# A linear-attention and sparse-FFN kernel: the attention's instruction order planned for all five engines, its q and k/v products interwoven, its division moved to ScalarE

## The chip, the cores and the metric

The kernel runs on one core of a Trainium2 chip. A core has a matrix engine (TensorE, PE in the profile), VectorE (DVE), ScalarE (ACT), GpSimd (POOL) and SyncE (SP), which here only issues DMAs. Each engine takes its instructions in the order in which the program was built, and waits where an operand isn't there yet; whatever stands behind the waiting instruction waits too. Matrix products are written to PSUM, eight banks of 128 x 512 float32 words; everything else lies in SBUF or in DRAM. The metric is the device time of one execution, in microseconds.

## What is computed

All values are float32. The input x has 2 batches of 1,024 positions with 512 features. The first layer is causal linear attention, the second an FFN whose hidden values are thinned 2 of 4; each is put between two layer norms and added to its input.

```python
q, k, v = xn @ Wq.T, xn @ Wk.T, xn @ Wv.T        # 16 query heads, 4 k/v heads, 128 wide
q, k = rope(q), rope(k)
qf, kf = elu(q) + 1, elu(k) + 1
state += kf outer v;  z += kf                     # running over the positions
out = (qf @ state) / (qf . z + 1e-6)
x = x + layernorm(out @ Wo.T)
h = silu(xn2 @ w_gate) * (xn2 @ w_up)             # 2,048 wide
h = h with the two largest of every four kept
x = x + layernorm(h @ w_down)
```

## The kernel before

**Tiling.** The attention runs in 16 steps, numbered `n`. A step takes 128 positions of both batches (`c = n % 8`) and one half of the heads (`n // 8`, two passes). Inside a step there are four groups `i`, each one batch with one k/v head and its four query heads. The FFN follows in four blocks of 512 positions.

**Products.** Each 2 x 2 block product (q, k/v, o, gate, up, down) is made with seven multiplications instead of eight, in the helper `strassen` (L121). It uses three PSUM banks: `cb` gathers products 1, 6, 7, 4; `ca` holds product 2; `ce` gathers 5 and 3. Between two products into `cb`, ScalarE copies the bank out (`keep`, L133), and VectorE later adds the copies to the other banks (L142, L155, L162). The next product into the same bank must wait for the copy. In the attention the banks come from one pool of four (`ps_mm`); transposes have a bank of their own (`ps_tr`), scores one (`ps_sc`), and the attention's numerators and denominators two (`ps_nm`).

**A step.** `kv_products(n)` and `q_products(n)` make k, v and q (L635), and `features` applies rope on VectorE (L656, L662), adds on GpSimd (L668), and makes elu + 1 with a relu and an exponential on ScalarE (L670, L671) and one VectorE operation (L672). A q block is then turned into the layout of its heads: `turned` transposes 32 x 32 blocks on VectorE (L581), `store_blocks` writes 256 KB to DRAM (L588), `load_blocks` reads them back in four DMAs (L593). `scores(n, i)` multiplies k and q (L740) and masks on VectorE (L749). `attend(n, i)` multiplies with the state and with v (L765, L766), makes the addition to the state (L769), and divides on VectorE (L771 to L774). Its result goes the same way through DRAM (`ob`), and `o_sums` and `o_products(n - 1)` make the output projection (L838) a step later. In the second pass both passes' outputs are added, normed and written to DRAM as `x2`.

**Preparation.** The seven-product scheme needs sums of weight blocks. Those of the second pass and of the FFN are made during the attention by `prepare` in small parts, one part per call of `first(i)`: it loads a unit of 1 MB on SyncE, makes four additions on GpSimd (L497 to L501), and stores seven pieces.

**What sets the order.** The attention runs inside `manual_schedule` for PE, Pool and SP: for these three engines the order is that of the program text, which is written out by hand with generators (`run(qpr, 2)` advances the q chain by two products). VectorE and ScalarE are left to the framework's scheduler, as are all engines in the FFN. In a step the order of the products is q1 q2 q6 q5 q7, attend, score, q4 k1 q3 k2 k6 k5 k7, attend, score, k4 k3, o1 o2 o6, attend, score, o5, the k transpose, o7, attend, score, o4 o3. The last FFN-like work inside the attention are two `gate` chains (`early`), which fill the last step.

Of the kernel before, what the change touches and what calls it, by code (L numbers as in the profile page):

```python
# [31 lines left out]
FACTORS = {1: (0, 0), 2: (1, 1), 3: (4, 2), 4: (2, 6), 5: (6, 3), 6: (3, 4), 7: (5, 5)}  # L32


@with_exitstack
def kernel(
# [369 lines left out]
    ps_mm = left("ps_mm", 4, space=PSUM)  # L406
    ps_tr = left("ps_tr", 1, space=PSUM)
# [74 lines left out]
    def prepare(units):  # L482


        loaded = prepare_load(*units[0])
        written = None
        yield
        for n in range(len(units)):
            (a11, a12, a21, a22), dst = loaded
            if written:  # L490
                written()
            for k, a in enumerate((a11, a12, a22)):
                nc.sync.dma_start(out=dst(k), in_=a)
            yield
            if n + 1 < len(units):
                loaded = prepare_load(*units[n + 1])
            nc.gpsimd.tensor_tensor(a22, a21, a22, ALU.add)  # L497
            nc.gpsimd.tensor_tensor(a21, a11, a21, ALU.subtract)
            yield
            nc.gpsimd.tensor_tensor(a11, a22, a11, ALU.subtract)  # L500
            nc.gpsimd.tensor_tensor(a12, a12, a11, ALU.subtract)  # L501

            def written(dst=dst, sums=(a11, a12, a21, a22)):
                for k, a in enumerate(sums):
                    nc.sync.dma_start(out=dst(3 + k), in_=a)

            yield
        written()

# [34 lines left out]
    def prepare_all():  # L544
        yield from sums(wo_sb, nc.gpsimd)
        units = []
        for quarter, t, parts in (
            (kv_quarter, wkv_dram, (slice(0, 2),)),
            (q_quarter, wq_dram, (slice(0, 1), slice(1, 2))),
            (o_quarter, wo_dram, (slice(0, 2), slice(2, 4))),  # L550
        ):
            for part in parts:
                units.append((quarters(quarter, part), view_quarters, part_of(t, part)))
        for jb in range(NJB):
            for i, w in enumerate((w_gate, w_up)):
                units.append((whole(columns(w, jb)), view_gu, into_gu(gu_dram[jb][i])))
        for jb in range(NJB):
            of = w_down[jb * 512 : (jb + 1) * 512, :].rearrange("(p r) o -> p r o", r=4)
            units.append((whole(of), view_d, into_d(jb)))
        yield from prepare(units)  # L560

    preparing = prepare_all()

    def transposed(src):

        t = ps_tr.tile([P, 4, P], F32, tag="tr", name="pst")
        for j in range(4):
            nc.tensor.transpose(t[:, j, :], src[:, j, :], ident)
        return t
# [7 lines left out]
    def turned(src):  # L577


        t = qp.tile([P, 4, 4, 32], F32, tag="blocks", name="blocks", bufs=4)  # L580
        nc.vector.transpose(  # L581
            out=t.rearrange("p b i r -> p i b r"),
            in_=src.rearrange("p i (b d) -> p i b d", d=32),
        )
        return t

    def store_blocks(t, to):
        nc.sync.dma_start(out=to, in_=t.rearrange("p b i r -> p (b i r)"))  # L588

    def load_blocks(t, of_):  # L590

        for b in range(4):
            nc.sync.dma_start(  # L593
                out=t[b * 32 : (b + 1) * 32],
                in_=of_.rearrange("(u d) (b e) -> b d u e", u=4, b=4)[b],
            )

    xf = {}

    def step_normalize(n):  # L600
        xns = []
        for b in range(B):
            mean, rs = layernorm_scale(xt[n][:, b, :], "a")
            normalize(xt[n][:, b, :], xt[n][:, b, :], mean, rs)
            xns.append(xt[n][:, b, :].rearrange("p (c d) -> p c d", c=NIC))
        return xns

    def step_input(n, xns, batches=range(B)):

        if 0 in batches:  # L610
            xf[n] = ln.tile([P, 7, 2, P], F32, tag="xf", name="xf")
        t = xf[n]
        for b in batches:
            pt = transposed(xns[b])
            if b == 0:
                nc.scalar.copy(t[:, 0:2].rearrange("p q k d -> p (q k) d"), pt)
            else:
                nc.vector.tensor_tensor(t[:, 3], pt[:, 0:2, :], t[:, 0], ALU.subtract)
                nc.scalar.copy(t[:, 2], pt[:, 2:4, :])
        if 1 in batches:  # L620
            nc.vector.tensor_tensor(t[:, 4], t[:, 2], t[:, 3], ALU.subtract)
            nc.vector.tensor_tensor(t[:, 5], t[:, 4], t[:, 0], ALU.subtract)
            nc.vector.tensor_tensor(t[:, 6], t[:, 1], t[:, 4], ALU.subtract)
            nc.sync.dma_start(out=xf_dram[n], in_=t)

    def step_input_again(n):
        t = ln.tile([P, 7, 2, P], F32, tag="xf", name="xf")
        nc.sync.dma_start(out=t, in_=xf_dram[n - NC])
        xf[n] = t

    def project(w, x_):
        def product(bank, i, start):
            wi, xi = FACTORS[i]
            for k in range(2):
                nc.tensor.matmul(  # L635
                    bank.rearrange("p h d -> p (h d)"),
                    x_[:, xi, k, :],
# [8 lines left out]
    def strassen_a(width, product, c11, c12, c22, done):  # L646
        return strassen((ps_mm, qp), [P, width // HD, HD], product, c11, c12, c22, done)

    def features(src, n, dst):
# [4 lines left out]
        u = rawp.tile([P, 4, HD], F32, tag="u", name="u")  # L654
        r = rawp.tile([P, 4, HD], F32, tag="r", name="r")
# [6 lines left out]
        nc.vector.tensor_tensor(  # L662
            r.rearrange("p h (t d) -> p h t d", t=2),
            src.rearrange("p h (t d) -> p h t d", t=2)[:, :, ::-1, :],
            sin,
            ALU.mult,
        )
        nc.gpsimd.tensor_tensor(u, u, r, ALU.add)  # L668

        nc.scalar.activation(r, u, AF.Relu, scale=-1.0)  # L670
        nc.scalar.activation(r, r, AF.Exp, scale=-1.0)  # L671
        nc.vector.scalar_tensor_tensor(dst, u, 0.0, r, ALU.max, ALU.add)  # L672
# [3 lines left out]
    kf, kT, v1, q_blocks = {}, {}, {}, {}  # L676
    GROUPS = ((0, 0), (1, 1), (0, 1), (1, 0))

    def kv_products(n):
        raw = rawp.tile([P, 4, HD], F32, tag="raw", name="kraw", bufs=4)  # L680
# [3 lines left out]
        yield from strassen_a(  # L684
            256,
            project(weights[n // NC][0], xf[n]),
            raw[:, 0:2, :],
            raw[:, 2:4, :],
            v[:, 2:4, 0:HD],
            lambda t: nc.scalar.copy(v[:, 0:2, 0:HD], t),  # L690
        )
        f = kv.tile([P, 4, HD], F32, tag="kf", name="kf")
        features(raw, n, f)
        kf[n] = f

    def k_transposed(n):
        t = kv.tile([P, 4, P], F32, tag="kT", name="kT")
        nc.scalar.copy(t, transposed(kf[n]))
        kT[n] = t

    def q_products(n):
        raw = [rawp.tile([P, REP, HD], F32, tag="raw", name="qraw", bufs=4) for _ in range(3)]

        def feature(i, src):
            f = qp.tile([P, REP, HD], F32, tag="qf", name="qf", bufs=1)
            features(src, n, f)
            q_blocks[n, i] = turned(f)

        run = strassen_a(
            512,  # L710
            project(weights[n // NC][1], xf[n]),
            raw[0],
            raw[2],
            raw[1],
            lambda t: feature(2, t),
        )
        for i, _ in enumerate(run):
            if i == 1:
                feature(0, raw[0])
            elif i == 4:  # L720
                feature(1, raw[1])
            elif i == 6:
                feature(3, raw[2])
            yield

    state = {}
    qT, am, o, blocks = {}, {}, {}, {}

    def q_store(n, i):
        store_blocks(q_blocks.pop((n, i)), qb_dram[n % 2][i])  # L730

    def q_load(n, i):
        t = qp.tile([P, 4, P], F32, tag="qT", name="qT", bufs=4)
        load_blocks(t, qb_dram[n % 2][i])
        qT[n, i] = t

    def scores(n, i):
        b, j = GROUPS[i]
        sc = ps_sc.tile([P, 4, REP, 32], F32, tag="sc", name="sc")
        nc.tensor.matmul(  # L740
            sc.rearrange("p u h t -> p (u h t)"),
            kT[n][:, 2 * b + j, :],
            qT[n, i].rearrange("p u e -> p (u e)"),
            start=True,
            stop=True,
        )
        t = qp.tile([P, 4, REP, 32], F32, tag="am", name="am")
        mask = causal.rearrange("p (u t) -> p u t", t=32).unsqueeze(2)
        nc.vector.tensor_tensor(t, sc, mask.broadcast_to([P, 4, REP, 32]), ALU.mult)  # L749
        am[n, i] = t  # L750

    def attend(n, i):

        b, j = GROUPS[i]
        c = n % NC
        v = v1[n][:, 2 * b + j, :]
# [5 lines left out]
        for u in range(4):  # L762
            dst = nmv[:, u // 2, u % 2, :]
            if c > 0:
                nc.tensor.matmul(dst, q[:, u, :], state[b, j], start=True, stop=False)  # L765
            nc.tensor.matmul(dst, a[:, u, :], v, start=(c == 0), stop=True)  # L766
        if c < NC - 1:
# [377 lines left out]
```

## Time and profile before

| | |
|---|---|
| median of three runs | 1433.1 us (1426.0 to 1436.2) |
| profiled execution | 1429.7 us, of which the span is 1428.0 us |
| mean granted TensorE clock | 0.971 |
| TensorE busy | 1313.1 us, 92% of the span |
| VectorE, ScalarE, GpSimd busy | 892.0, 402.1, 336.0 us |
| moved by DMA | 263 MB, 184 GB/s |
| the costliest wait of TensorE | `PE cb L635 <- ACT u L133`: 27.2 us in 23 waits |

A busy matrix engine isn't an engine at its pace: matmuls are pipelined, and the time shown for one is longer than the distance to the next. The distance between two starts is what counts. The clock is given as a share of full speed; a stage at 0.5 runs its products at half speed.

### The profile page before, as it was taken

To read this page: it belongs to the slowest core of one execution; us is meant where nothing else is said; L and a number is where in the kernel's file an instruction comes from. 1 tells how busy PE (TensorE), PEld (TensorE's weight loads), DVE (VectorE), ACT (ScalarE), POOL (GpSimd) and SP (SyncE) were. 2 spreads that over 40 slices of the span, in tenths; PEclk is the share of its full clock that TensorE was granted. 3 is DMA by queue.
4 is the path that set the end of the run, shared out by engine and by line. 5 is a ranking of instruction groups with operands and counts; after the bars stand their busy time and mean duration, and the time that the engine had idled before them with its cause. 6 is when DMAs were issued, how large, how long until landed. Compare 5 with 4: busy or idle time off the path is not lost.

```text
span 1428.0 us, 17352 instructions
## 1 busy us (share of the span) xinstructions
PE 1313.1 (92%) x5888; PEld 1033.9 (72%) x5888; DVE 892.0 (62%) x1612; ACT 402.1 (28%) x698; POOL 336.0 (24%) x265
## 2 busy tenths in 40 slices
PE   5889989899789878898898999999999999999997
PEld 3456757666566566576566888888888888888886
DVE  5767875676466557667767548734774278525762
ACT  3523332232122212222232332403331242213311
POOL 5333332332233323435341220101001100110000
PEclk9889999999989999999999999999999999999999
DMA  6256666666776886676557437445553655356412
GB/s 222 93 172 202 213 207 220 197 199 205 250 259 217 248 262 190 210 243 212 182 197 257 164 126 244 140 142 207 155 154 118 229 156 153 123 173 176 113 60 89
DMA packets 200295, 263.32 MB, mean 184 GB/s; under 512 B 18448, under 2 KB 125968, under 8 KB 196112
## 3 DMA queue, kind: packets, MB, share of 16 engines
q1 hardware_dynamic: 198976, 260.38, 57.0%
q10 hardware_dynamic: 1232, 1.84, 0.4%
q8 instruction: 48, 0.79, 0.2%
q14 instruction: 39, 0.32, 0.1%
HBM read 178.52 MB, written 83.62 MB: 184 GB/s over the span
## 4 chain that ended last, share of the span: by engine, by line
PE 64%; DVE 16%; DMA 5%; ACT 5%; issue 4%; POOL 3%; SPq 3%; DVEq 0%; ACTq 0%; POOLq 0%
PE cb L237 15%; PE ce L237 8%; PE cb L346 6%; PE cb L838 6%; PE cb L635 5%; PE ca L237 4%; PE ce L346 4%; POOL u L668 3%; PE nm L766 3%; DVE blocks L581 2%; PE nm L765 2%; PE ce L838 2%; DVE r L662 2%; PE sc L740 2%; PE ce L635 2%
## 5 line engine op out<-in xcount | busy, mean ns | idle before, releaser
L133 ACT COPY u<-cb 128x512 f32<-128x512 f32 (+1 forms) x252 | 126.0, 500 | 553.4 <-PE cb L237 189.5
L668 POOL TENSOR_TENSOR u<-u,r 128x512 f32<-128x512 f32 x80 | 106.0, 1326 | 308.8 <-DVE r L662 240.4
L635 PE MATMUL cb<-wq,xf 128*128 128x512 f32 x256 | 128.5, 626 | 23.5 <-DMA xf<-xf 8.3
L838 PE MATMUL cb<-wo,of 128*128 128x256 f32 x512 | 124.9, 388 | 9.6 <-DVE of L825 8.3
L237 PE MATMUL cb<-fxt,wgu 128*128 128x256 f32 x512 | 117.8, 381 | 1.9 <-ACT u L133 1.9
L838 PEld LDWEIGHTS cb<-wo,of 128*128 128x128 f32 x512 | 97.1, 194 | 30.9 <-issue 12.3
L237 PE MATMUL cb<-fxnT,wgu 128*128 128x256 f32 x512 | 116.9, 379 | 0.0
L635 PEld LDWEIGHTS cb<-wq,xf 128*128 128x128 f32 x256 | 49.6, 199 | 83.8 <-issue 65.9
L237 PEld LDWEIGHTS cb<-fxt,wgu 128*128 128x128 f32 x512 | 96.5, 190 | 17.7 <-ACT u L133 4.4
L237 PEld LDWEIGHTS cb<-fxnT,wgu 128*128 128x128 f32 x512 | 97.2, 190 | 13.6 <-issue 0.5
L766 PE MATMUL nm<-v,am 128*128 128x129 f32 x512 | 101.0, 289 | 2.1 <-ACT state L787 2.1
L185 POOL TENSOR_TENSOR h<-h 128x512 f32<-128x512 f32 x16 | 23.3, 1459 | 332.1 <-DVE ht L182 297.4
L765 PE MATMUL nm<-state,qT 128*128 128x129 f32 x448 | 92.1, 289 | 0.0
L670 ACT ACTIVATE r<-u 128x512 f32<-128x512 f32 x80 | 50.2, 630 | 148.8 <-POOL u L668 106.3
L635 PE MATMUL cb<-wkv,xf 128*128 128x256 f32 x256 | 73.4, 413 | 19.9 <-ACT u L133 19.9
L155 DVE TENSOR_TENSOR y<-u,ce 128x256 f32<-128x256 f32 (+1 forms) x21 | 9.5, 459 | 128.3 <-ACT u L133 128.3
L672 DVE SCALAR_TENSOR_TENSOR qf<-u,r 128x512 f32<-128x512 f32 x64 | 58.2, 910 | 48.4 <-ACT r L671 43.4
L766 PEld LDWEIGHTS nm<-v,am 128*128 128x128 f32 x512 | 82.4, 206 | 3.8 <-ACT state L787 2.5
L635 PEld LDWEIGHTS cb<-wkv,xf 128*128 128x128 f32 x256 | 50.4, 203 | 47.1 <-ACT u L133 28.0
L765 PEld LDWEIGHTS nm<-state,qT 128*128 128x128 f32 x448 | 77.5, 206 | 9.2 <-issue 6.8
L740 PE MATMUL sc<-qT,kT 128*128 128x512 f32 x128 | 67.2, 607 | 1.3 <-DMA qT<-qb 1.3
L346 PE MATMUL cb<-wd,h 128*128 128x256 f32 x256 | 58.3, 381 | 4.4 <-DVE h L325 4.3
(150 smaller groups left out, 2487.1 us busy)
## 6 DMA issues: line engine op xcount, KB each, us to landing
wgu<-gs SPq DMA_DIRECT2D x112, 256.0 KB, 2.7
wgu<-us SPq DMA_DIRECT2D x112, 256.0 KB, 2.7
wd<-d_dram SPq DMA_DIRECT2D x28, 1024.0 KB, 4.9
qb<-blocks SPq DMA_DIRECT2D x64, 256.0 KB, 2.8
qT<-qb SPq DMA_DIRECT2D x256, 64.0 KB, 2.3
ob<-blocks SPq DMA_DIRECT2D x60, 256.0 KB, 3.0
of<-ob SPq DMA_DIRECT2D x240, 64.0 KB, 2.0
xf<-xf SPq DMA_DIRECT2D x16, 896.0 KB, 5.3
```

The source lines that it names most:

```text
L133: nc.scalar.copy(t, b)
L237: nc.tensor.matmul(bank[:, j, :], w[:, k, j, :], xf[xi][:, k, :], start=(start and j == 0 and k == 0), stop=(j == 1 and k == 1), skip_grou ...
L346: nc.tensor.matmul(bank[j] if split else bank[:, j, :], hf[jb][hi][:, k, j * P : (j + 1) * P], w[:, jb, k, :], start=(start and jb == 0 an ...
L581: nc.vector.transpose(out=t.rearrange("p b i r -> p i b r"), in_=src.rearrange("p i (b d) -> p i b d", d=32),)
L635: nc.tensor.matmul(bank.rearrange("p h d -> p (h d)"), x_[:, xi, k, :], w[:, wi, k, :], start=(start and k == 0), stop=(k == 1), skip_grou ...
L668: nc.gpsimd.tensor_tensor(u, u, r, ALU.add)
L670: nc.scalar.activation(r, u, AF.Relu, scale=-1.0)
L672: nc.vector.scalar_tensor_tensor(dst, u, 0.0, r, ALU.max, ALU.add)
L740: nc.tensor.matmul(sc.rearrange("p u h t -> p (u h t)"), kT[n][:, 2 * b + j, :], qT[n, i].rearrange("p u e -> p (u e)"), start=True, stop= ...
L765: nc.tensor.matmul(dst, q[:, u, :], state[b, j], start=True, stop=False)
L766: nc.tensor.matmul(dst, a[:, u, :], v, start=(c == 0), stop=True)
L838: nc.tensor.matmul(bank.rearrange("p h d -> p (h d)"), of[n, xi][:, k, :], w[:, wi, k, :], start=(start and k == 0), stop=(k == 3), skip_g ...
```

## The change

**A plan.** A class `Plan` walks through the attention when the kernel is built. It keeps a clock and, for each engine, the time from which it is free. Small generators describe what must happen after a product (`yield "dve", 0.75` means that VectorE is taken for 0.75 us; `yield "of", n, i` waits for a named event; a third element is a rank among requests of the same time). The instruction is issued to the program when its turn comes in this plan, and that fixes the order on VectorE, ScalarE, GpSimd and SyncE. TensorE's order is still written out, and `plan.pe` only moves the clock. The whole attention is now under `manual_schedule` for all five engines. Nothing of the plan is left when the kernel runs.

```diff
+class Plan:
+    def step(self):
+        t, rank, _, process, request = heapq.heappop(self.heap)
+        if request:
+            engine, length = request[:2]
+            if self.free.get(engine, 0.0) > t:
+                self.push(self.free[engine], rank, process, request)
+                return
+            t += length
+            self.free[engine] = t
+        self.now = t
+        self.go_on(process)
+    def pe(self, length, issue, *names):
+        self.need(*names)
+        start = max([self.pe_free] + [self.ready[name] for name in names])
+        self.until(start)
+        issue()
+        self.now = self.pe_free = start + length
...
-    with tc.manual_schedule(
-        engines={mybir.EngineType.PE, mybir.EngineType.Pool, mybir.EngineType.SP}
-    ):
+    with tc.manual_schedule(engines={E.PE, E.Pool, E.SP, E.DVE, E.Activation}):
```

**Banks by role.** The four banks and the transposes' one become one `a`, two `b` and two `e` banks. `chain` takes the place of `strassen` in the attention, with the same seven products in the same order; transposes of x, of k and of the last outputs use an `a` or an `e` bank.

```diff
-    ps_mm = left("ps_mm", 4, space=PSUM)
-    ps_tr = left("ps_tr", 1, space=PSUM)
+    ps_mm = left("ps_mm", 2, space=PSUM)
...
+    def bank(kind, shape):
+        bufs = 1 if kind == "a" else 2
+        k = uses[kind]
+        uses[kind] += 1
+        before = [("bank", kind, k - bufs)] if k >= bufs else []
+        plan.need(*before)
+        t = ps_mm.tile([P, 512], F32, tag=f"mm{kind}", name=f"c{kind}", bufs=bufs)
...
+        def snapshot(b, i):
+            yield "act", act, 0
+            kept[i] = keeps[0].tile(shape, F32, tag=keeps[1], name=f"u{i}", bufs=keeps[2])
+            nc.scalar.copy(kept[i], b)
+            plan.signal((*name, "kept", i))
```

**Blocks through DRAM.** Turning, storing and loading are one generator. The plan takes 0.1 us of SyncE for the store and 0.45 us for the four loads, and lets 2.6 us pass between them.

```diff
+    def moved(src, through, new, name, *names):
+        yield "dve", 0.75
+        t = qp.tile([P, 4, 4, 32], F32, tag="blocks", name="blocks", bufs=4)
+        nc.vector.transpose(
...
+        yield 0.1
+        yield "sp", 0.1
+        nc.sync.dma_start(out=through, in_=t.rearrange("p b i r -> p (b i r)"))
+        yield 2.6
+        for n in names:
+            yield n
+        yield "sp", 0.45
+        t = new()
         for b in range(4):
             nc.sync.dma_start(
```

**Division on ScalarE.** One VectorE multiplication over 128 x 512 becomes four ScalarE activations over 128 x 128, each with a column of reciprocals as its scale.

```diff
-        nc.vector.tensor_tensor(
-            t.rearrange("p (i j) d -> p i j d", i=2),
-            nmv[:, :, :, 0:HD],
-            den.unsqueeze(3).broadcast_to([P, 2, 2, HD]),
-            ALU.mult,
-        )
+            for u in range(4):
+                yield "act", 0.37
+                nc.scalar.activation(
+                    t[:, u, :],
+                    nmv[:, u // 2, u % 2, 0:HD],
+                    AF.Copy,
+                    scale=den[:, u // 2, u % 2 : u % 2 + 1],
+                )
```

**The step's order.** The q and k/v chains of the next step are interwoven product by product (the lines for steps after the first):

```diff
+            kvp, qpr = kv_products(n + 1), q_products(n + 1)
+            run(qpr, 1)
+                run(kvp, 1)
+                run(qpr, 1)
+                run(qpr, 1)
+            run(kvp, 1)
+                outputs(0)
+            run(kvp, 1)
+            run(qpr, 1)
+            run(kvp, 1)
+            run(qpr, 1)
+            run(kvp, 1)
+                outputs(1)
+                run(qpr, 1)
+                run(kvp, 1)
+                run(qpr, 1)
+                run(kvp, 1)
+                run(opr, 2)
+                outputs(2)
+                run(opr, 2)
+                k_transposed(n + 1)
+                run(opr, 1)
+            outputs(3)
```

`outputs(i)` releases one part of the preparation, then attends to group i and makes the next group's scores. The last two products of the o chain open the next step. The first step (n = 0) and the last have orders of their own; in the last, `early_gate` makes the two gate chains, interwoven with the last two o chains.

**Smaller parts.** The norms of the two batches (of the four blocks at the FFN's beginning) share one square root on ScalarE (`layernorm_pair`). `features` works in place on the raw block, with three buffers for `r`. The reloaded x factors of the second pass are requested at the start of a step, for the step after next. The second pass's weights are requested every 3.5 us of the plan once the first pass's last q (k/v) products have been issued. The FFN after the attention's end is unchanged in the text.

## What was expected of it

> **What bounds the kernel now.** I read the stages first, then the waits of TensorE, then one step of it in order of time, then SyncE's queue and its DMAs. In the stages I cut the span at the end of the start-up (88 us, where the first product of the third step's q begins), at the same product 13 steps later (733.8) and at the end of the attention's last product (848).
>
> ```profile
> 0.00:88.03 88.03, 63.16 (x195) 37.75 (x195) 58.70 (x103) 34.77 (x60) 39.04 (x33) 0.86 0.48 156
> 88.03:733.79 645.76, 578.49 (x2549) 416.65 (x2548) 426.54 (x803) 176.41 (x337) 219.84 (x176) 0.96 0.68 219
> 733.79:848.00 114.21, 106.49 (x523) 86.63 (x522) 67.43 (x149) 38.47 (x71) 22.76 (x19) 0.99 0.52 176
> 848.00:1428.00 580.00, 564.99 (x2625) 492.86 (x2623) 339.37 (x558) 152.41 (x231) 54.40 (x39) 1.00 0.49 152
> ...
> PE cb L635 <- ACT u L133: 27.2, 23, 5.5
> PE ce L635 <- DVE r L662: 14.3, 10, 2.8
> PE pst L568 <- DVE x L119: 9.6, 3, 7.8
> ```
>
> The columns of a stage are its length, the busy time of TensorE, its weight loads, VectorE, ScalarE and GpSimd, then the granted clock, the DMA share and GB/s. The last stage, 580 us, runs at clock 1.00 and back to back; the change hardly touches it, so I leave it at 580. The attention's 848 us are where something can be won. Busy time doesn't say how much, since matmuls overlap in it; I take the pace from starts in the timeline of one step.
>
> ```profile
> 143.42 1.88 PE L635 MATMUL cb<-wq,xf 128*128 128x512 f32 x4
> 145.14 0.39 PE L765 MATMUL nm<-state,qT 128*128 128x129 f32 x2
> ...
> 147.15 1.02 PE L740 MATMUL sc<-qT,kT 128*128 128x512 f32 x2
> 148.01 1.88 PE L635 MATMUL cb<-wq,xf 128*128 128x512 f32 x4
> 149.73 1.03 PE L635 MATMUL cb<-wkv,xf 128*128 128x256 f32 x4
> 150.59 1.88 PE L635 MATMUL ce<-wq,xf 128*128 128x512 f32 x4
> ...
> 154.04 1.13 PE L635 MATMUL cb<-wkv,xf 128*128 128x256 f32 x4 [0.70 <-ACT u L133]
> ...
> 157.57 1.13 PE L635 MATMUL cb<-wkv,xf 128*128 128x256 f32 x4 [1.05 <-ACT u L133]
> ...
> 163.13 0.60 PE L568 MATMUL pst<-ident,x 128*128 128x128 f32 x4
> 163.57 1.89 PE L838 MATMUL cb<-wo,of 128*128 128x256 f32 x8
> 165.30 1.89 PE L838 MATMUL ca<-wo,of 128*128 128x256 f32 x8
> ```
>
> A q product takes 1.72 us (148.01 to 149.73), a k/v product 0.86, an o product 1.73, an attend 2.01 (145.14 to 147.15), a score 0.86, four transposes 0.44. A step holds 7 of each product, 4 attends, 4 scores and one k transpose: 12.0 + 6.0 + 12.1 + 8.0 + 3.4 + 0.4 = 42.1 us, and 0.9 more where x is transposed. With the lighter attends around the change of pass (no state to read at its first step, none to write at the last) the 13 steps sum to 547 us. They took 645.8, or 49.7 a step. Of the 99 us between, the timeline's brackets add up to 67 us of waiting, and a clock of 0.96 is 26 us. So TensorE is the bound, and a seventh of the attention is waiting and the clock dips that follow it. The start-up loses 25 us to waits (9 of them before the first product, which stay) and 12 to its clock of 0.86; the tail about 10.
>
> **The clock, row and rule.** The rows show clock losses only in stages that have waits (0.86, 0.96, 0.99 against 1.00). The Trainium skill's "TensorE: Matmul & The Clock Gate", section "Why this matters for your kernels", has the clock fall to half only after an idle gap of more than some 3 us. By that rule only the long waits (5.5, 7.9 and 7.3 us, beside a few near 3) cost clock, and some 10 of the 26 us would come back. The rows speak for more: the window from 672 to 714 us has no wait above 2.8 us and a clock of 0.92. I count the clock in proportion to the waits that go, which is some 18 us of the 64 below; by the rule it would be 10, and the forecast 8 us higher.
>
> **The change, part by part.**
>
> *TensorE's order.* No product is added. What changes is how much other TensorE work lies between a product and the bank it waits for. Before, k7 came one product (k5, 0.86 us) after k6, whose copy it waits for; the copy takes 0.37 us, on a ScalarE that often stood behind an addition of GpSimd. Hence most of the 27.2 us, and the 14.3 us come from k5's bank, released by VectorE. Afterwards the steady order is q1 k1 q2 q6 k2, attend, score, k6 q5 k5 q7 k7, attend, score, q4 k4 q3 k3 o1 o2, attend, score, o6 o5, transpose, o7, attend, score, o4 o3. Between q1 and q6 lie 2.6 us, between k6 and k7 4.3, between k7 and k4 4.6. The tightest is k2 behind q2 on the one "a" bank: 1.72 us against an addition of 0.68. Two attends, which share the one nm bank pair, lie at least 6 us apart but in the first step. So the 67 us of waits lose their cause, if VectorE and ScalarE keep the planned order.
>
> *Division on ScalarE.* It takes 64 operations of 0.685 us (the o<-nm,den row, L774) off VectorE, 2.7 us a step, and VectorE falls from 426.5/13 = 32.8 to 30.1 us a step. ScalarE gets 16 a step of 128x128. The nearest row is the state copy of 128x129 out of PSUM, 0.263 us: 4.2 us, from 13.6 to 17.8 us a step. "ScalarE: Activation LUTs", section "What ACT_TABLE_LOAD costs", prices an activation with a pointer operand at 0.28 us + 0.83 ns an element, 0.39 us here: 6.2 us a step. Neither makes ScalarE a bound; I take the row. A bank copy behind four divisions is 1.1 to 1.6 us late, which the gaps above cover. Without that cover (a copy behind a relu that waits for GpSimd) it is worth 1 to 5 us each time, as the 5.5 us wait was.
>
> *Norms in pairs, fewer table switches.* One square root for two blocks saves 0.3 us of ScalarE each. Off the path; nothing.
>
> *SyncE.* This is where I expect the gain to be limited. Every q and o block goes through DRAM: a store of 256 KB, then four loads that SyncE can't issue before the store has landed.
>
> ```profile
> L593 SPq DMA_DIRECT2D of<-ob x240: 302/430/1496, 74.7 to 792.2; - x120
> ...
> SPq L588 <- DVE blocks L581: 134.1, 43, 9.8
> SPq L593 <- DMA ob<-blocks: 59.5, 24, 6.8
> ```
>
> An issue costs 0.43 us (the median in the first row), and the changed kernel has, like this one, 57.8 DMAs a step (752 in 13 steps, counted in its SyncE order): 25 to 26 us. The plan reckons 0.1 us for one and 0.45 for four. "DMA: Bandwidth & Descriptors" has the same view: its table of the fixed cost gives dispatch some 50 ns, and "Issuing engines are not separate DMA queues" calls the time to initiate usually small. By that SyncE spends 3 us a step and can't matter; by the row it spends 26. I go by the row. Worse, before only 26 of the 124 loads of a block stood four DMAs or fewer behind their store; afterwards 83 do, 44 of them directly behind it. In the 13 steps before, 24 such loads waited 59.5 us, 2.5 each. Afterwards 71 of them, 5.5 a step: 13.7 us. SyncE then needs 26 + 13.7 = 40 us of a TensorE step of 42.1. On top come its waits for VectorE's blocks, 134.1/13 = 10.3 us a step before. Those were largely spare time, and a SyncE that runs late finds its blocks done. I keep half, 5: 44.8 us a step. The bounds are 42.5 (none stays, TensorE decides) and 50.1 (all stay).
>
> *Bank roles (1 + 2 + 2 instead of 4, transposes included).* The o chain's first bank is the q chain's of the same step, released by two rope products (1.4 us) 3.4 us earlier. Covered; without cover 0 to 1 us a step, within the bounds above.
>
> *GpSimd and the preparation.* The same additions at the same one part per attend, but attends come 11 instead of 12.4 us apart, and stores of prepared weights had kept GpSimd idle up to 16.7 us. I put nothing on it, since its queue was then mostly empty; up to 1 us a step if rope additions queue behind it.
>
> *Start.* The first score needs q's first block through DRAM: 0.68 + 1.6 rope + 1.33 GpSimd + 0.63 + 1.28 table + 0.63 + 0.90 + 0.70 transpose + 3.0 store + 1.8 issues + 2.3 landing = 15 us, against 18.6 us of products that now lie between. GpSimd still makes wq's sums then (four of 2.47 us), and three VectorE operations stand ahead, so I leave a wait of 3 us and other small ones; of the 28 us lost after the first product 16 come back. The tail gives 4 of its 10.
>
> Sum: 13 x (49.7 - 44.8) = 64, + 16 + 4 = 84 us. The profiled execution took 1429.7 us (span 1428.0): 1346. The median of the runs, 1433.1, lies 3.4 above it: 1349.
>
> **Rivals.**
>
> *All waits go* (chance 0.22): SyncE's waits for VectorE vanish and steps take 42.6. 13 x 7.1 = 92, + 20 + 6 = 118: 1315. For it: one step before took 42.7 us (its second q product at 436.93, the next step's at 479.65). Against: that was the light step, without states, of 38.5 us work.
>
> *SyncE or DMA clearly the bound* (0.20): steps of 47.5, start + 8, tail 2: 39 us, 1394. For it: the DMA share, 0.68 at 49.7 us a step, would be 0.75 at 45, and landings lengthen (of 3.0 us typical, 9.7 seen).
>
> *Slower* (0.10): the waits for landings come on top of those for VectorE, none replaced, in SyncE's queue. A step is then 26 + 10.3 + 5.5 w. It reaches 49.7 plus the 20 us of start and tail (1.5 a step) at w = 2.7 us, only 0.2 over the measured 2.5. At w = 3.2, with every load directly behind its store, 53.9: 13 x 4.2 - 20 = 35 us, 1468. Against: SyncE would have to stay just as late as its producers.
>
> *The order planned isn't the order that helps* (0.06): ScalarE stands behind GpSimd as often as before and only the interleaving counts, steps of 49 and start + 2: 11 us, 1422.
>
> **How the numbers follow.** The forecast has 0.42. The range takes in the first rival down to 1305 and the second up to 1418; outside lie the slower case, half of the last, and a little below. About 1% is what a measurement of this kernel can tell from no change: faster 0.84, same 0.05, slower 0.11.
>
> **What would show it.** Right: waits of TensorE in the 13 steps under 30 us, clock 0.98 or more; SyncE's waits for ob and qb landings well over 150 us, for blocks well under 134; VectorE near 30 us a step; divisions near 0.26 us. Wrong, if TensorE waits for qT or of (SyncE the bound), or if copies still wait behind relu.

## The result, and the profile after

The changed kernel takes 1471.5 us (median of 4 runs, 1469.7 to 1473.4) where the kernel before takes 1431.6 (4 runs). The ratio is 1.028, with a 95% interval of 1.024 to 1.032: slower, where faster was forecast. The profiled execution took 1473.4 us, with a span of 1471.7.

First the stages, cut at the same places of the program as before; the columns are those of the prediction.

```profile
0.00:76.10 76.10, 55.80 (x190) 34.15 (x191) 56.40 (x89) 30.52 (x63) 39.00 (x33) 0.93 0.51 169
76.10:775.80 699.70, 586.02 (x2555) 430.26 (x2554) 407.66 (x751) 237.93 (x542) 229.72 (x178) 0.91 0.64 205
775.80:890.00 114.20, 104.92 (x513) 85.78 (x512) 64.84 (x135) 41.07 (x92) 26.27 (x20) 0.96 0.51 168
890.00:1471.70 581.70, 567.28 (x2633) 494.23 (x2632) 337.94 (x556) 154.82 (x232) 50.64 (x36) 1.00 0.49 152
```

The start became 12 us shorter. The 13 steps in the middle became 54 us longer: 53.8 us each instead of 49.7, with VectorE less busy than before and TensorE's clock down to 0.91. Tail and FFN stand where they were. So the whole loss lies in the middle, and no engine there is busier than TensorE at 84%.

Next, what TensorE waits for in the 13 steps, the costliest first: total, times, longest.

```profile
PE ca L866 <- DVE qraw L710: 61.5, 4, 20.7
PE cb L866 <- ACT u L703: 36.6, 8, 6.7
PE sc L1018 <- DMA qT<-qb: 7.9, 1, 7.9
PE cb L1186 <- ACT v L945: 5.9, 4, 2.4
```

The many short waits of before (23 of 1.2 us on copies, 10 of 1.4 on k5's bank) are gone, as forecast. In their place stand twelve long ones at the same two kinds of release: a bank that VectorE reads (L710) or ScalarE copies out (L703). Neither engine is slow; the same stretch of the waits of all engines says what holds them.

```profile
DVE of L1160 <- DMA of<-ob: 133.0, 12, 18.0
ACT o L1080 <- DVE den L1076: 129.3, 42, 9.7
...
SPq L776 <- DMA ob<-blocks: 100.9, 37, 6.6
SPq L769 <- DVE blocks L763: 99.2, 33, 10.9
SPq L776 <- DMA qb<-blocks: 73.5, 33, 5.9
```

L1160 is the first of the three sums that `o_sums` makes for the output projection. It needs the attention output of group 3, the last group of the step, after that block's way through DRAM. It was nearly always late: 12 waits in 13 steps, 11 us each (a thirteenth, 24.9 us at the change of pass, is put down to a weight load; the sums' waits in the whole execution are 158 us). In the kernel before, the same sum (L825) never waited for over 0.05 us. The rows give the wait instructions in front of it, in ns: shortest, median, longest; first the kernel before, then the changed one (one wait of VectorE can be split over several of them).

```profile
L825 DVEq EVENT_SEMAPHORE  x16: 21/35/50, 115.7 to 801.9; - x16
L1160 DVEq EVENT_SEMAPHORE  x35: 21/50/18151, 106.2 to 836.1; - x35
```

The fence before that has two more engines. ScalarE's division (L1080) waits for the reciprocals of VectorE (L1076). SyncE (L776, the four loads of a block) waits 174 us for stores to land.

One step in order of time shows how these hang together: VectorE, then TensorE, then SyncE's queue (start, length, instruction; in brackets the idle time before it and what ended it).

```profile
331.77 0.71 DVE L763 STREAM_TRANSPOSE blocks<-o 128x512 f32<-128x512 f32 x1 [0.36 <-ACT o L1080]
333.86 0.42 DVE L710 TENSOR_TENSOR y<-u,ce 128x256 f32<-128x256 f32 x1 [1.38 <-PE ce L1186]
352.23 0.69 DVE L1160 TENSOR_TENSOR of<-of 128x512 f32<-128x512 f32 x1 [17.95 <-DMA of<-ob]
352.84 0.68 DVE L710 TENSOR_TENSOR qraw<-u,ca 128x512 f32<-128x512 f32 x1
...
337.95 1.88 PE L866 MATMUL cb<-wq,xf 128*128 128x512 f32 x4
353.58 2.07 PE L866 MATMUL ca<-wkv,xf 128*128 128x256 f32 x4 [13.74 <-DVE qraw L710]
355.44 0.64 PE L1062 MATMUL nm<-state,qT 128*128 128x129 f32 x2
...
334.67 0.42 SPq L769 DMA_DIRECT2D ob<-blocks  x1
...
338.72 1.79 SPq L776 DMA_DIRECT2D qT<-qb  x4
340.62 0.37 SPq L839 DMA_DIRECT2D xf<-xf  x1
341.03 0.43 SPq L847 DMA_DIRECT2D xf<-xf  x1
341.56 0.83 SPq L769 DMA_DIRECT2D ob<-blocks  x1
...
348.77 1.74 SPq L776 DMA_DIRECT2D of<-ob  x4
```

Follow group 3's block. VectorE has it transposed at 332.5. SyncE stores it only at 341.6, because it works through, and waits in, the loads of other blocks first: 9.1 us. The loads are issued 7.2 us later, when the store has landed, and the sum starts at 352.2. The plan gives this way 0.1 + 0.1 + 2.6 + 0.45 + 2.8, or 6 us (the last is for the loads to land); it took 19.7. For 18 of these VectorE stood at the sum, and directly behind it in its queue stood the addition that frees q's one "a" bank. k2 needs that bank, so TensorE waited 13.7 us. The bank was covered by a distance of one product; the queue in front of its release was not.

In eight other steps the same sum stands elsewhere in the order, and the loss takes the way over ScalarE. From a step of that kind:

```profile
199.88 0.69 DVE L1160 TENSOR_TENSOR of<-of 128x512 f32<-128x512 f32 x1 [8.88 <-DMA of<-ob]
...
202.15 0.15 DVE L1074 TENSOR_SCALAR den<-nm 128x4 f32<-128x4 f32 x1
202.34 0.18 DVE L1076 RECIPROCAL den<-den 128x4 f32<-128x4 f32 x1
...
202.61 0.89 ACT L1080 ACTIVATE o<-nm,den 128x128 f32<-128x128 f32 x3 [7.45 <-DVE rs L799]
203.37 0.38 ACT L703 COPY u<-cb 128x256 f32<-128x256 f32 x1
203.81 2.07 PE L866 MATMUL cb<-wkv,xf 128*128 128x256 f32 x4 [4.45 <-ACT u L703]
```

Here the reciprocals stand behind the sum, ScalarE stands at its division for want of them, and a bank's copy stands behind the division. (The row names `rs` of L799 as what ended ScalarE's wait. It ended at the same time as the reciprocals of L1076, which are what the division reads.) Three engines wait for one landing. All twelve long waits of TensorE follow this pattern: it went on 1.3 us after the sum had started in the four that go over VectorE, and 3.0 or 3.9 us after in the eight that go over ScalarE.

### The profile page after: what moved, and what is told of

It is laid out like the page before. It is cut to its first block, busy times and chain, and to the rows that moved or that the text cites. A ratio compares the mean times of both kernels' runs of the same rounds, so it can differ in the third digit from the quotient of the medians.

```text
span 1471.7 us, 17413 instructions
## 1 busy us (share of the span) xinstructions
PE 1314.0 (89%) x5888; PEld 1044.4 (71%) x5888; DVE 866.8 (59%) x1529; ACT 464.3 (32%) x929; POOL 345.6 (23%) x265
## 4 chain that ended last, share of the span: by engine, by line
PE 67%; DMA 13%; DVE 8%; SPq 6%; issue 2%; ACT 2%; POOL 1%; DVEq 0%; ACTq 0%; POOLq 0%
PE cb L308 14%; PE ce L308 7%; DMA ob<-blocks 6%; PE cb L866 6%; PE cb L1186 6%; PE cb L417 6%; SPq L776 4%; PE ca L308 4%; PE ce L417 4%; PE nm L1063 3%; DMA qb<-blocks 3%; PE ce L866 3%; PE ce L1186 3%; PE nm L1062 3%; PE sc L1018 2%
## 5 line engine op out<-in xcount | busy, mean ns | idle before, releaser
L204 ACT COPY u<-cb 128x512 f32<-128x512 f32 x102 | 59.4, 583 | 308.7 <-PE cb L308 176.7
L1080 ACT ACTIVATE o<-nm,den 128x128 f32<-128x128 f32 x256 | 78.7, 369 | 201.2 <-DVE den L1076 143.7
L907 POOL TENSOR_TENSOR qraw<-qraw,r 128x512 f32<-128x512 f32 x48 | 62.3, 1299 | 262.3 <-DVE qraw L898 230.6
L703 ACT COPY u<-cb 128x256 f32<-128x256 f32 (+1 forms) x150 | 67.5, 451 | 177.6 <-PE cb L866 141.5
L866 PE MATMUL cb<-wq,xf 128*128 128x512 f32 x256 | 122.1, 600 | 0.0
L866 PE MATMUL cb<-wkv,xf 128*128 128x256 f32 x256 | 76.0, 424 | 39.6 <-ACT u L703 36.6
L866 PEld LDWEIGHTS cb<-wkv,xf 128*128 128x128 f32 x256 | 53.0, 212 | 77.7 <-ACT u L703 43.2
L1160 DVE TENSOR_TENSOR of<-of 128x512 f32<-128x512 f32 x16 | 11.2, 703 | 158.0 <-DMA of<-ob 133.1
L638 POOL TENSOR_TENSOR wraw<-wraw 128x512 f32<-128x512 f32 x68 | 95.6, 1405 | 29.7 <-DMA gs<-wraw 11.7
L1062 PE MATMUL nm<-state,qT 128*128 128x129 f32 x448 | 97.2, 302 | 0.2 <-DVE state L1103 0.2
L1063 PEld LDWEIGHTS nm<-v,am 128*128 128x128 f32 x512 | 86.4, 215 | 4.0 <-ACT o L1080 3.6
L1062 PEld LDWEIGHTS nm<-state,qT 128*128 128x128 f32 x448 | 81.6, 217 | 6.7 <-issue 3.0
L866 PEld LDWEIGHTS cb<-wq,xf 128*128 128x128 f32 x256 | 49.0, 193 | 46.6 <-issue 45.0
```

Source lines behind the costliest of these rows:

```text
L204: nc.scalar.copy(t, b)
L638: nc.gpsimd.tensor_tensor(to, i0, i1, op)
L703: nc.scalar.copy(kept[i], b)
L866: nc.tensor.matmul(bank.rearrange("p h d -> p (h d)"), xf[n][:, xi, k, :], w[:, wi, k, :], start=(start and k == 0), stop=(k == 1), skip_g ...
L1080: nc.scalar.activation(t[:, u, :], nmv[:, u // 2, u % 2, 0:HD], AF.Copy, scale=den[:, u // 2, u % 2 : u % 2 + 1],)
```

## The experiments

The sums' part of the plan, which most experiments touch:

```python
def o_sums(n):
    for i in (3, 0, 1, 2):
        yield "of", n, i            # planned landing of group i's block
    if n > 0:
        yield "o", n - 1, 4
    ...
    yield "dve", 0.75               # the sum at L1160
    nc.vector.tensor_tensor(of[n, 3], of[n, 3], of[n, 0], ALU.subtract)
```

The theory: the sums stand too early in VectorE's fixed order, because the plan counts the block's way through SyncE too short. The rivals: the division on ScalarE ties the engines together; SyncE's standing is itself the bound; the DMAs are late because of large transfers; other figures of the plan are wrong. In the table, each for the whole execution, "sums wait" is what L1160 (or its counterpart) waits for DMAs, "SyncE" what SyncE waits for stores of q and o blocks to land, and "k" what the k transpose waits for k's features.

| kernel | us | ratio to before, 95% | sums wait | SyncE | k |
|---|---|---|---|---|---|
| changed kernel | 1471.5 | 1.028 (1.024 to 1.032) | 158.0 | 190 | 0.2 |
| sums 12 us later | 1410.2 | 0.983 (0.980 to 0.986) | 4.0 | 155 | 47.9 |
| SyncE's figures | 1390.7 | 0.969 (0.965 to 0.972) | 74.8 | 79 | 0.3 |
| both | 1406.6 | 0.980 (0.977 to 0.983) | 0.5 | 84 | 44.1 |
| SyncE's figures, sums 5 us later | 1367.9 | 0.954 (0.950 to 0.958) | 26.8 | 88 | - |
| sums 5 us later alone | 1433.0 | 1.000 (0.998 to 1.003) | 92.8 | 222 | 2.6 |

**The sums later.**

```diff
+        if n + 1 < STEPS:
+            yield 12.0
         if n > 0:
             yield "o", n - 1, 4
```

> The sums of the output factors are asked for 12 us later in the plan; nothing else is edited, and SyncE's order, its issues and its waits for landings are nearly the same. If the loss comes from VectorE standing at the first sum (L1160) until the last block has landed, with the bank releases behind it: VectorE's wait at that line falls from 158 us to under 50, TensorE's waits in the 13 steps from some 140 to under 50, and the time to 1370 to 1400 us. If SyncE's throughput is the bound, the wait moves to TensorE's own wait for factors or qT and the time stays above 1450.

It took 1410.2 us. The 61 us that came back are all of the loss and more, while SyncE still waited 155 us for landings. So the place of the sums is a cause, and SyncE's standing alone is not. It missed the 1370 to 1400 expected, and TensorE's waits in the 13 steps fell to 57 us, not under 50 (in the changed kernel they were 113, not the 140 that the expectation says). The wait that took the place of the old ones:

```profile
PE ca L683 <- DVE kf L915: 47.9, 13, 9.4
```

```profile
294.17 0.68 DVE L1162 TENSOR_TENSOR of<-of 128x512 f32<-128x512 f32 x1
294.88 0.69 DVE L1165 TENSOR_TENSOR of<-of 128x512 f32<-128x512 f32 x1
...
298.45 0.42 DVE L710 TENSOR_TENSOR kraw<-u,ce 128x256 f32<-128x256 f32 x1 [0.18 <-PE ce L866]
...
303.86 1.76 DVE L890 TENSOR_TENSOR r<-kraw,rope 128x512 f32<-128x512 f32 x1
...
311.75 0.65 DVE L915 SCALAR_TENSOR_TENSOR kf<-kraw,r 128x512 f32<-128x512 f32 x1
```

The first fence is TensorE's costliest wait, the second VectorE in one step. The sums now don't wait, but they stand among the additions of the q and k chains, and k's rope (L890) is made 5.4 us after k's last addition (298.45), behind q's; the k transpose, which TensorE has in its fixed order, comes too early for it.

**SyncE's real figures.** 0.43 us for an issue and 1.75 for four are the measured lengths of these instructions.

```diff
-        yield "sp", 0.1
+        yield "sp", 0.43
-        yield 2.6
+        yield 3.4
-        yield "sp", 0.45
+        yield "sp", 1.75
```

(0.43 at the other single DMAs of the plan too, 1.75 or 0.43 for the preparation's loads.)

> Only the plan's figures for SyncE change: 0.43 us an issue instead of 0.1, 1.75 for four loads instead of 0.45, 3.4 us instead of 2.6 from store to load. If the plan's wrong figures for SyncE are the cause, the order comes out with fewer loads directly behind their stores and the sums later: SyncE's waits for ob and qb landings fall from 174 to under 90 us and the time to 1370 to 1410. If the lateness comes from transfers of 1 MB standing ahead in the DMA queues, the change helps less: 1430 to 1460.

1390.7 us, with the sums untouched but planned from later landings. They still wait 75 us. The two edits together, in one kernel:

> Both edits: sums 12 us later and SyncE's true figures in the plan. If the two causes are one (the block is late, and VectorE waits for it), the result is close to the better of the two alone, within 15 us. If they add, it is 20 us or more below both, near 1350.

1406.6, worse than the figures alone by 16 us and in neither of the two expected places: the sums no longer wait (0.5 us), but the k transpose waits for k's features again (44.1 us). It looks as if two corrections of one lateness push the sums past their place.

**The sums later by 5 us**, with SyncE's figures, and without them:

> SyncE's true figures in the plan, and the sums 5 us later instead of 12. With 12 us they came among the rope operations of k and held up its transpose (44 us of waits there). If both kinds of wait are only a matter of where the three sums stand in VectorE's queue, 5 us avoids most of both: 1370 to 1388. If the sum stands wrong wherever it is put, since SyncE delivers its block at varying times, it stays at 1390 to 1405.

> The changed kernel with the sums 5 us later and SyncE's figures as they were. The block comes some 8 to 18 us later than VectorE asks for it, so 5 us takes part of each wait: VectorE's wait at the first sum 158 to some 80 us, time 1405 to 1440. If the place among the rope operations is all that counts, it comes near the 1368 of the version with true figures.

With the figures 1367.9 us, 4.6% under the kernel before and the fastest of all. Its start and its 13 steps, then VectorE in the step that answers to the one above:

```profile
0.00:79.44 79.44, 56.95 (x197) 35.02 (x197) 62.83 (x98) 33.09 (x70) 40.26 (x34) 0.96 0.59 194
79.44:663.44 584.00, 559.43 (x2556) 409.37 (x2555) 405.99 (x744) 236.02 (x538) 234.34 (x177) 0.99 0.77 242
```

```profile
310.02 0.67 DVE L763 STREAM_TRANSPOSE blocks<-o 128x512 f32<-128x512 f32 x1
310.62 0.65 DVE L1162 TENSOR_TENSOR of<-of 128x512 f32<-128x512 f32 x1
...
322.03 0.42 DVE L710 TENSOR_TENSOR kraw<-u,ce 128x256 f32<-128x256 f32 x1
322.49 0.69 DVE L890 TENSOR_TENSOR r<-kraw,rope 128x512 f32<-128x512 f32 x1
...
327.34 1.75 DVE L915 SCALAR_TENSOR_TENSOR kf<-kraw,r 128x512 f32<-128x512 f32 x1
```

The sums come without a wait, earlier in the step, and k's rope follows its addition at once. The steps take 44.9 us at a clock of 0.99, with the same work on every engine as in the slow kernel (VectorE 406 us here, 408 there). Without the figures the same delay gives 1433.0: the sums wait 93 us. SyncE waits 222 us for landings there, more than the 190 of the changed kernel, and yet the time is 38 us shorter. With no figures corrected, delays of 0, 5 and 12 us give 1471, 1433 and 1410.

**The division back on VectorE**, in the changed kernel and in the fastest one:

```diff
-            for u in range(4):
-                yield "act", 0.37
-                nc.scalar.activation(...)
+            yield "dve", 0.69, 0
+            nc.vector.tensor_tensor(..., den..., ALU.mult)
```

> The division goes back to one VectorE operation, all else as changed. If the ScalarE division is part of the loss (a chain of den, four activations, transpose that is longer than one VectorE operation), the time falls by 10 to 25 us, to 1447 to 1461. If the loss is VectorE's wait for landings alone, the division hardly matters: 1465 to 1480, since VectorE has time to spare while it waits.

> The version with true SyncE figures and sums 5 us later (1368 us), with the division back on VectorE. If VectorE's load matters once it no longer stands at the sums (2.7 us more a step, TensorE at 46 us a step), the time rises 10 to 30 us, to 1378 to 1398. If the division was worth its 9 us only as a shorter way to the block, or is hidden, it stays within 5 us of 1368.

1480.3 (ratio to before 1.032, 1.028 to 1.036) and 1392.7 (0.974, 0.973 to 0.976). In the changed kernel the division's place makes no clear difference, and with it on VectorE the "a" bank simply waits more often (`PE ca L866 <- DVE qraw L710`: 79.6 us in 8). So the division on ScalarE passes the wait on, but it isn't its cause. In the fastest kernel, taking it back costs 25 us. That isn't VectorE's load alone: the plan puts the operations in another order with it, and the k transpose's wait for k's features is back (29.0 us in 10 waits, none before), so what the place of the division alone is worth stays open.

**SyncE's own standing.** With SyncE's figures, the plan's time from a store to its loads was raised from 3.4 to 5.0 us.

> SyncE's true figures, and 5.0 us from store to load instead of 3.4, as landings behind a transfer of 1 MB showed up to 7.2 us. If late landings are what is left, SyncE's waits for landings fall from 74 to under 40 us in the 13 steps, VectorE's wait at the sum from 73 to under 40, and the time to 1370 to 1388. If not, 1388 to 1400.

1388.3 us (0.969, 0.965 to 0.973), the same as with 3.4. SyncE's waits in the whole execution, and the sum's:

```profile
SPq L769 <- DVE blocks L763: 150.1, 55, 11.6
...
SPq L776 <- DMA ob<-blocks: 26.3, 13, 4.3
...
SPq L776 <- DMA qb<-blocks: 9.2, 7, 2.1
...
DVE of L1160 <- DMA of<-ob: 49.5, 8, 13.2
```

Its waits for landings fell from 79 to 36 us and nothing came of it. Much of it became waiting for blocks, 150 us instead of 124: SyncE has time to spare. The sums' waits fell too, from 75 to 57 us (49.5 above and 7.1 put down to another load), short of the 40 expected, and that brought nothing clear either, so the length of the sums' wait alone doesn't give its cost. The same figure together with the 5 us for the sums:

> True figures, sums 5 us later, and 5.0 us from store to load. SyncE's waits for landings fall to some 35 us from 83. If SyncE's standing at its landings costs anything once VectorE no longer waits, 1350 to 1362; if it is spare, as in the version without the 5 us (1388 against 1391), 1362 to 1375.

1398.0 us (0.977, 0.974 to 0.979), a miss. SyncE waits only 38 us for landings, yet it is 30 us slower than the fastest, with k's features late once more (34.5 us in 12 waits, against none). As with the 12 us, the sums seem to have been pushed too far.

**The large transfers.** In the changed kernel the preparation's loads and the x factors' 0.9 MB stores and loads were issued from ScalarE's queue instead (for example):

```diff
-            yield "sp", 0.1
-            nc.sync.dma_start(out=xf_dram[n], in_=t)
+            yield "act", 0.05
+            nc.scalar.dma_start(out=xf_dram[n], in_=t)
```

> The plan's figures stay as they were; the loads of the preparation and the two transfers of the x factors (0.9 to 1 MB each time) are issued by ScalarE on its own queue, so that no block's store stands behind them and SyncE has some 4 us of issuing less a step. VectorE's order is the same but for two places. If the blocks are late because of SyncE's queue, VectorE's wait at the first sum falls from 158 us to under 110 and the time to 1410 to 1445. If the order alone decides, 1465 or more.

1473.3 us (1.028, 1.024 to 1.031). SyncE still waits 176 us for landings (190 in the changed kernel) and the sums 153 (158). In the step shown, two 0.9 MB transfers stood just ahead of the late store; issuing such transfers through SyncE is not what makes the sums wait. Whether the transfers themselves slow a store, whoever issues them, isn't tested: they were still made, and 14 of the 60 `ob` stores still took over 4 us to land (15 in the changed kernel).

**The plan's other figures.** The last feature operation at 0.9 us, the table switch at 1.28, norms 0.75, the division 0.29, GpSimd 1.33 and 1.4, besides SyncE's figures; then also with the 5 us.

> All figures of the plan that the traces contradict by over a tenth are corrected: SyncE's as before, the last feature operation 0.9 us, a table switch of 1.28 us after each square root, normalize 0.75, a division 0.29, the x factors' sums 0.5, GpSimd's additions 1.33 and 1.4. If the plan's other errors cost as SyncE's did, the time falls 10 to 25 us below 1391. If SyncE's were the only ones that matter, 1385 to 1400.

> All corrected figures and sums 5 us later. If the other figures are worth nothing beside the place of the sums (as 1390 against 1391 says), within 8 us of 1368. If they help once the sums are out of the way, 1345 to 1360.

1390.4 (0.970, 0.966 to 0.974) and 1373.9 (0.961, 0.959 to 0.962): no gain over SyncE's figures alone in either place.

## Why the prediction was wrong

**The step that failed** is the last sentence on TensorE's order: "So the 67 us of waits lose their cause, if VectorE and ScalarE keep the planned order." They kept it, and that was the harm: TensorE waited 113.4 us in the 13 steps, where under 30 was forecast, at a clock of 0.91, and a step took 53.8 us instead of 44.8. The distances worked out there (1.72 us from q2 to k2 against an addition of 0.68, and so on) are right. But they are distances to the operation that frees a bank, not to the queue in front of it. On VectorE any operation that waits for something slow holds every release behind it. The framework's scheduler, which ordered VectorE in the kernel before, had put the sums where they never waited; the plan, with too short a way for the block, put them where they did. The prediction followed the blocks through DRAM as far as SyncE and TensorE and named, as signs of being wrong, TensorE waiting for qT or `of`. It didn't ask who on VectorE reads `of`.

**SyncE** came out nearly as reckoned: landing waits 174 us (178 forecast, 13.7 a step), waits for blocks 99 (65 forecast, half of 134). The 0.43 us an issue, which the prediction took from its row, held; the 50 ns of dispatch that it weighed against it stand, in "DMA: Bandwidth & Descriptors", in a section on DMAs that GpSimd issues. 26 us of issue (the forecast's figure), 13.4 and 7.6 make 47 a step, while the steps took 53.8. That leaves 7 us of a step, and with the sums moved by 5 us alone SyncE waited longer in a faster kernel: its standing was not what set the steps. Its real part was to make one block late.

**The slower rival** had the number, 53.9 us a step and 1468, and the wrong place. It made SyncE the bound. Against that speak the run that was 38 us faster with longer landing waits (222 us for 190), and the run with its landing waits cut from 79 to 36 us without gain. That the number fits is luck.

**The clock** was counted in proportion to the waits, as 26 us in the 13 steps before. Of the 55 us at half clock there, 13 lay inside waits, where they cost nothing, so the cost was nearer 21. In the changed kernel half clock came during or just after each of the thirteen waits over 3 us and ended 3.0 to 5.9 us after the wait, with no relation to its length. The first two rows below start at the ends of waits of 4.26 and 13.74 us; the granted clock is the third figure from the end.

```profile
254.13:257.10 2.97, 2.97 (x10) 2.56 (x11) 2.94 (x5) 1.07 (x3) 2.81 (x3) 0.50 0.00 0
353.58:359.50 5.92, 5.92 (x23) 5.56 (x24) 3.16 (x5) 1.26 (x2) 3.81 (x3) 0.50 0.85 232
113.73:117.15 3.42, 3.09 (x7) 2.52 (x8) 3.42 (x7) 3.09 (x6) 1.27 (x1) 0.50 0.18 70
```

Outside the waits the 13 steps have 65 us at half clock, a loss of 33. With the 113.4 us of waits that is 146 of the 152.7 us by which the steps (699.7) exceed the forecast's pure work (547); the rest isn't accounted for. In proportion to the waits, 26 us for 67, the clock would have cost 44. The rule that the prediction set against it, that of the Trainium skill's "TensorE: Matmul & The Clock Gate", section "Why this matters for your kernels", no idle gap over some 3 us, fits these thirteen waits. It isn't all of it: the third row shows half clock at the end of a wait of 2.40 us (at 114.06) and for 3.1 us after it, and the kernel before has a clock of 0.92 from 672 to 714 us without a wait above 2.8.

**Other terms.** Against the profiled sum of 1346 us, the profiled execution is 127 longer: 118 in the 13 steps (699.7 for 582), 4 in the start (12 us won, not 16), 4 in the tail (nothing won), 2 in the FFN. VectorE fell to 31.4 us a step (30.1 forecast). The division's record is 369 ns, near the 0.39 that the prediction had from "ScalarE: Activation LUTs" and not the 0.26 that it took:

```profile
L1080 ACT ACTIVATE o<-nm,den 128x128 f32<-128x128 f32 x256 | 78.7, 369 | 201.2 <-DVE den L1076 143.7
```

Yet three in a row take 0.89 us, so in a queue one costs about 0.26. That the price didn't matter stands: it is the wait in front of it that counts.

With the sums in their place a step takes 44.9 us, the 44.8 of the forecast, in another make-up: SyncE waits 88 us for landings there in the whole execution, not the 190 of the changed kernel, so that agreement is partly chance.

**Open.** Delays of 0, 5 and 12 us were tried and none between. Why SyncE's real figures and the 5 us do better together than any single edit isn't settled: the sums' wait explains much of the order (158 us at 1471, 93 at 1433, 75 at 1391, 27 at 1368) but not all of the 42 us between the kernels with 93 and 75, nor why the kernel with 57 is no faster than the one with 75. The k wait, which comes back where the sums are put later, was read from the order of VectorE and not isolated. The interwoven chains and the banks by role were not tried alone.

## What to carry to other kernels

When you fix an engine's order by hand or by a plan, look in its queue for every operation that waits for a transfer, and list what stands behind it: bank releases and reciprocals behind a late sum cost TensorE more than all the short waits that the new order removed. A plan is as good as its figure for the slowest route; here it was the issue and landing of DMAs (0.1 us planned, 0.43 measured), and correcting those few figures and moving three operations by 5 us turned 2.8% slower into 4.6% faster. Such a place is a window: too early waits for the transfer, too late stands in the way of the next chain.

## What the runs showed of the hardware

A 256 KB store landed 7.2 us after its issue where two 0.9 MB transfers had been issued in the microsecond before, against 2.2 us as the median of such stores in the whole execution; that the one caused the other is not shown. During or just after each of the thirteen waits over 3 us (3.6 to 20.7) in the changed kernel's 13 steps the granted clock of the matrix engine fell to 0.50, and it stayed there until 3.0 to 5.9 us after the wait's end, with no relation to the wait's length. And scaled activations of 128 x 128 in a row overlap: 369 ns each by the record, three in 0.89 us.
